# Two bottleneck layers in fp32: a Gram matrix whose pixels are transposed by transfers and VectorE instead of TensorE, a 3x3 row combination with four products, and filters made on GpSimd

## The chip, the cores and the metric

One core of one Trainium2 chip. The metric is device time in microseconds (us) of one execution, the median of several. Most executions of one kernel agree within 0.3%. The profiled span is some 2 us shorter than the timed run.

## The reference

Two equal layers act on x of 64 x 1024 x 14 x 14 fp32. The convolution biases and the residual scale are inputs (zero here, and softplus of zero is 0.69).

```python
def _bn(x, gamma, beta):
    mean = jnp.mean(x, axis=(0, 2, 3), keepdims=True)
    var = jnp.var(x, axis=(0, 2, 3), keepdims=True)
    ...
out = jax.nn.relu(_bn(_conv(x, w1, b1, 1, 0), g1, be1))     # 1x1, 1024 -> 256
out = jax.nn.relu(_bn(_conv(out, w2, b2, 1, 1), g2, be2))   # 3x3, 256 -> 256
out = _bn(_conv(out, w3, b3, 1, 0), g3, be3)                # 1x1, 256 -> 1024
out = jax.nn.softplus(residual_scale)[0] * out
return jax.nn.relu(x + out)
```

Each batch normalisation needs the statistics of all 64 images before anything can be normalised, so the work falls into stages: first convolution; 3x3 convolution of layer 0; its Gram stage; statistics, third convolution and residual of layer 0 fused with the first convolution of layer 1; 3x3 convolution and Gram stage of layer 1; its third convolution and residual.

## The kernel before

The mean and variance of the third convolution are not taken from its outputs. They follow from the Gram matrix (the products of every channel with every other, summed over pixels) of its 256 input channels over 12,544 pixels. For that product the kernel lays the pixels on the partitions, while the activations `y_all` have channels on the partitions. So TensorE transposes 98 chunks of 128 pixels, VectorE takes a constant off on the way out of PSUM, and TensorE multiplies.

```python
CH = 2;  NT = NPX // (CH * P);  NZT = 4       # two chunks of 128 pixels per step
FOUR = 3, 4                                   # row combinations with four products

def gram(psum, pool, aff, crow, beside):
    ...
    def products(k, zt):
        for c in range(CH):
            nc.tensor.matmul(g0, zt[:, c, 0:P], zt[:, c, :], ...)
            nc.tensor.matmul(g1, zt[:, c, P:M], zt[:, c, P:], ...)
    for k in range(NT):
        ...                                   # norms of the next image group (ScalarE)
        tp = psum.tile(CH * M)
        for c in range(CH):
            for s in range(MS):
                nc.tensor.transpose(tp[...], y_all[:, s, px], ident)
        zt = zts[k % NZT]
        nc.vector.tensor_tensor(zt[:, :, :M], tp..., crow..., ALU.subtract)
        if before is not None:
            products(*before)
        if k in beside:
            beside[k]()                       # layer 0: one piece of layer 1's filters
        before = k, zt
```

The 3x3 filters are turned into six row combinations, in four pieces per layer. Pieces of layer 0 are made during the first stage in a part of `y_all` not yet written; pieces of layer 1 during the Gram stage of layer 0, in two buffers borrowed from the pool that holds the x tiles.

```python
def filters(b, s, o, spare):
    first, second = spare
    ...
    nc.sync.dma_start(out=g, in_=w2s[b][:, s, o])            # SyncE loads the raw filter
    nc.vector.tensor_add(even, g[:, 0], g[:, 2])             # arithmetic: VectorE ...
    nc.scalar.activation(even, even, AF.Copy, scale=-1.0/6)  # ... and ScalarE
    ...
    nc.gpsimd.dma_start(out=us[b][i][:, s, o], in_=u)        # GpSimd stores each combination
```

The scheduler may move instructions when the program is built. SyncE's queue holds all loads of x. The kernel before gives the pieces of layer 0 two places in turn.

## Time and profile before

PE stands for TensorE's matmuls in the profile, PEld for its weight loads, DVE for VectorE, ACT for ScalarE, POOL for GpSimd, SP for SyncE, and a q after a name for that engine's queue. The granted clock is the share of full speed at which TensorE was let run. An issue is the instruction by which a queue starts a transfer, and the transfer lands when its data have arrived. A stage is measured from its first matmul to its last.

| stage (stretch of matmuls) | us |
|---|---|
| first convolution (ends at 310.99) | 305.3 |
| 3x3, layer 0 / layer 1 | 307.1 / 307.7 |
| Gram, layer 0 / layer 1 | 95.0 / 90.3 |
| statistics and fused stage | 625.0 |
| residual stage, layer 1 | 351.1 |
| kernel: 2118.75 (2117.68 to 2119.07), profiled span | 2116.9 |

The first lines are the busy tenths of TensorE and the granted clock in 40 slices of the span, from the page of the kernel before; the line after them is the first stage from its busy times by stretch, where the columns after the length are the busy times of PE, PEld, DVE, ACT and POOL, then the granted clock, the DMA share and GB/s.

```profile
PE   8999989999989999999999999899999899999999
...
PEclk9999999999999999999999999999999999999999
```

```profile
0.00:311.00 311.00, 302.10 (x904) 170.80 (x904) 194.20 (x273) 50.76 (x109) 13.79 (x30) 1.00 0.55 200
```

TensorE works through every slice at full clock.

### The profile page before, as it was taken

What the parts mean: (1) busy time and instruction counts of PE and PEld (TensorE: products, weight loads), DVE (VectorE), ACT (ScalarE), POOL (GpSimd) and SP (SyncE); (2) the same over time, 40 slices, a digit from 0 to 9 for tenths busy, and PEclk for the clock granted to TensorE, in tenths of its full rate; (3) what the DMA queues carried; (4) which work ended last, traced back from release to release, by engine and by line L of the source; (5) the groups of instructions that cost most, each with busy time, mean ns of one, the idle gap of its engine ahead of it and who ended that gap; (6) DMA issues with size and microseconds to landing.
All of it is one profiled execution on the core that took longest, in us unless ns stands there. A gap on an engine that the chain in (4) does not pass through costs nothing.

```text
span 2116.9 us, 27185 instructions
## 1 busy us (share of the span) xinstructions
PE 2068.3 (98%) x10368; PEld 1747.9 (83%) x10368; DVE 1433.2 (68%) x2778; ACT 814.2 (38%) x1579; POOL 243.5 (12%) x342
## 2 busy tenths in 40 slices
PE   8999989999989999999999999899999899999999
PEld 4555549999989889999999999799999897555555
DVE  5766559988866666666766667798888544444444
ACT  2211115233226055555555555523223402444444
POOL 0100000000001023333333333000000000000000
PEclk9999999999999999999999999999999999999999
DMA  7665425555543434444444443355554402778785
GB/s 292 250 211 209 163 90 192 201 191 184 200 159 118 155 150 159 177 183 161 175 160 176 183 160 145 120 214 184 190 208 180 194 1 99 306 277 325 282 321 215
DMA packets 45011, 400.00 MB, mean 189 GB/s; under 512 B 5584, under 2 KB 5840, under 8 KB 12240
## 3 DMA queue, kind: packets, MB, share of 16 engines
q1 hardware_dynamic: 30528, 280.28, 37.0%
q0 software_dynamic: 8448, 66.07, 7.7%
q10 hardware_dynamic: 5904, 51.91, 5.9%
q8 instruction: 82, 1.34, 0.3%
q14 instruction: 49, 0.40, 0.1%
HBM read 280.79 MB, written 117.44 MB: 188 GB/s over the span
## 4 chain that ended last, share of the span: by engine, by line
PE 93%; DVE 3%; ACT 2%; DMA 1%; issue 1%; POOL 0%; SPq 0%; DVEq 0%; ACTq 0%
PE ps L155 17%; PE ps L573 17%; PE ay L155 14%; PE ps L550 8%; PE cy L155 8%; PE ap L155 8%; PE ax L155 4%; PE cp L155 4%; PE ps L560 3%; PE cp L755 3%; PE cx L155 2%; PE ap L756 2%; ACT y L427 1%; PE ps L773 1%; DMA y<-in_w 0%
## 5 line engine op out<-in xcount | busy, mean ns | idle before, releaser
L573 PE MATMUL ps<-r,u 128*128 128x224 f32 (+1 forms) x2048 | 391.2, 343 | 14.1 <-DVE r L506 14.1
L573 PEld LDWEIGHTS ps<-r,u 128*128 128x128 f32 x2048 | 372.1, 190 | 18.9 <-DVE r L506 7.9
L155 PE MATMUL ps<-y,w 128*128 128x392 f32 x1024 | 340.5, 496 | 0.0
L155 PEld LDWEIGHTS ps<-y,w 128*128 128x128 f32 x1024 | 195.9, 191 | 143.5 <-issue 2.8
L837 DVE SCALAR_TENSOR_TENSOR x<-ps,scale,x 128x392 f32<-128x392 f32 x256 | 160.0, 626 | 175.5 <-PE ps L155 171.8
L265 ACT ACTIVATE cu<-cy,scale 128x196 f32<-128x196 f32 x372 | 154.0, 423 | 221.2 <-PE cy L155 221.2
L838 ACT ACTIVATE x<-x,shift 128x392 f32<-128x392 f32 x264 | 163.6, 622 | 183.7 <-DVE x L837 183.7
L155 PE MATMUL ay<-at,w1s 128*128 128x196 f32 (+1 forms) x752 | 209.7, 382 | 1.2 <-ACT au L265 1.0
L605 ACT ACTIVATE ms<-ps 128x448 f32<-128x448 f32 (+1 forms) x80 | 40.5, 506 | 333.7 <-PE ps L550 323.3
L155 PEld LDWEIGHTS ay<-at,w1s 128*128 128x128 f32 x752 | 136.0, 190 | 36.6 <-ACT au L265 4.6
L550 PE MATMUL ps<-sums,u 128*128 128x224 f32 (+1 forms) x768 | 158.6, 337 | 0.0
L265 ACT ACTIVATE x<-x,shift 128x392 f32<-128x392 f32 x248 | 140.9, 614 | 28.3 <-POOL x L399 28.3
L399 POOL TENSOR_TENSOR x<-x,cu 128x392 f32<-128x392 f32 x124 | 125.9, 1015 | 188.1 <-DVE x L373 188.0
L373 DVE SCALAR_TENSOR_TENSOR x<-cp,scale,x 128x196 f32<-128x196 f32 x248 | 103.4, 417 | 63.7 <-PE cp L155 63.7
L550 PEld LDWEIGHTS ps<-sums,u 128*128 128x128 f32 x768 | 131.5, 189 | 0.1
L155 PE MATMUL cy<-ct,w3s 128*128 128x196 f32 x496 | 123.0, 330 | 1.4 <-ACT cu L265 1.4
L755 PE MATMUL cp<-zt 128*128 128x257 f32 x392 | 120.6, 389 | 2.9 <-DVE zt L775 2.4
L265 ACT ACTIVATE au<-ay 128x196 f32<-128x196 f32 (+1 forms) x141 | 53.8, 381 | 167.2 <-PE ay L155 164.6
L155 PE MATMUL ap<-x,w1s 128*128 128x196 f32 (+1 forms) x376 | 107.7, 390 | 5.4 <-DVE y L311 5.4
L427 ACT ACTIVATE y<-y,shift,scale 128x1568 f32<-128x1568 f32 (+2 forms) x68 | 103.6, 1584 | 5.6 <-DVE shift L934 5.6
L155 PE MATMUL ax<-x,w 128*128 128x196 f32 (+1 forms) x376 | 104.8, 381 | 0.0
L155 PE MATMUL ay<-x,w 128*128 128x196 f32 (+1 forms) x376 | 104.8, 381 | 0.0
(226 smaller groups left out, 3429.2 us busy)
## 6 DMA issues: line engine op xcount, KB each, us to landing
x<-in_x SPq DMA_DIRECT2D x62, 1568.0 KB, 6.6
u<-u SPq DMA_DIRECT2D x64, 1280.0 KB, 5.5
x<-mid SPq DMA_DIRECT2D x32, 1568.0 KB, 7.6
mid<-x ACTq DMA_DIRECT2D x31, 1568.0 KB, 5.1
out<-x POOLq DMA_DIRECT2D x31, 1568.0 KB, 7.1
u<-u SPq DMA_DIRECT2D x32, 1024.0 KB, 4.8
u<-y POOLq DMA_DIRECT2D x16, 320.0 KB, 6.2
u<-spare POOLq DMA_DIRECT2D x16, 320.0 KB, 2.7
```

Source lines behind the costliest of these rows:

```text
L155: tc.keep_in_program_order(nc.tensor.matmul(*args, **kw))
L265: tc.keep_in_program_order(nc.scalar.activation(*args, **kw))
L373: nc.vector.scalar_tensor_tensor(v, bank, self.scale[:, o : o + 1], v, ALU.mult, ALU.add)
L399: nc.gpsimd.tensor_add(v, v, self.u12)
L427: nc.scalar.activation(y, y, AF.Relu, bias=shift[:, s : s + 1], scale=scale[:, s : s + 1])
L550: nc.tensor.matmul(to[:, o, :n], u[:, s, o, k], v[:, s].rearrange("p l c -> p (l c)"), start=(s == 0), stop=(s == MS - 1),)
L560: nc.tensor.matmul(to, u[:, s, o, k], v, start=(s == 0), stop=(s == MS - 1))
L573: nc.tensor.matmul(to, u[:, s, o, k], v, start=start, stop=stop, skip_group_check=by_slot)
L755: nc.tensor.matmul(g0, zt[:, c, 0:P], zt[:, c, :], start=first, stop=last)
L756: nc.tensor.matmul(g1, zt[:, c, P:M], zt[:, c, P:], start=first, stop=last)
L837: nc.vector.scalar_tensor_tensor(v, ps, scale[:, o : o + 1], v, ALU.mult, ALU.add)
L838: nc.scalar.activation(v, v, AF.Relu, bias=shift[:, o : o + 1])
```

## The change

Its intent: take 91 of the 98 chunk transposes off TensorE in each Gram stage. Sixteen transfers per tile of seven chunks rearrange 32-partition blocks within SBUF (block j of source i goes to block i, place j), and VectorE transposes inside 32x32 blocks. Besides that, the third row combination gets four products instead of five, the difference tiles of the 3x3 stages (differences of column halves, which a combination with four products needs) go to GpSimd, and so does all filter arithmetic. All four pieces of layer 0 now share one place. The core of the diff:

```diff
-CH = 2
-NT = NPX // (CH * P)
+CH0, CH = 7, 7
+QPX = (NPX - CH0 * P) // 4
+SPX = CH * P // 4
+NT = QPX // SPX                      # 13 tiles
-FOUR = 3, 4
+FOUR = 3, 4, 5
 def filters(b, s, o, spare):
     nc.sync.dma_start(out=g, in_=w2s[b][:, s, o])
-    ... (VectorE and ScalarE)
+    eng = nc.gpsimd
+    eng.tensor_tensor(even, g[:, 0], g[:, 2], ALU.add)
+    ... (31 more additions and scalings on eng)
-            nc.gpsimd.dma_start(out=us[b][i][:, s, o], in_=u)
+            eng.dma_start(out=us[b][i][:, s, o], in_=u)
-                    nc.vector.tensor_sub(diffs, r[:, :, :, :WH], r[:, :, :, WH:])
+                    nc.gpsimd.tensor_sub(diffs, r[:, :, :, :WH], r[:, :, :, WH:])
 def gram(...):
+        def spread(k):
+            px = slice(k * SPX, (k + 1) * SPX)
+            for s in range(MS):
+                norm(s, runs[:, s, :, px], aff)
+            to = sums_tile(homes, ("w1", "w3")[k % 2])...
+            for i in range(4):
+                for j in range(4):
+                    nc.sync.dma_start(
+                        out=to[32 * i : 32 * i + 32, :, j, :], in_=runs[32 * j : 32 * j + 32, :, i, px]
+                    )
+        def transposed(k, zd):
+            nc.vector.transpose(zt[:, :, :M]..., zd...)
+            nc.vector.tensor_sub(zt[:, :, :M], zt[:, :, :M], crow...)
...
-                if t % 4 == 2 and t // 4 < MS * MS:
+                if t % 6 == 2 and t // 6 < MS * MS:          # when a filter piece starts, first stage
```

## The prediction

> **What bounds the kernel now.** I read the page first: the busy line, then the chain of work that ended last.
>
> ```profile
> PE 2068.3 (98%) x10368; PEld 1747.9 (83%) x10368; DVE 1433.2 (68%) x2778; ACT 814.2 (38%) x1579; POOL 243.5 (12%) x342
> ...
> PE 93%; DVE 3%; ACT 2%; DMA 1%; issue 1%; POOL 0%; SPq 0%; DVEq 0%; ACTq 0%
> ```
>
> TensorE is busy for 98% of the span and holds 93% of the chain. So time is won by taking matmuls away, as long as nothing slower takes their place. The second view is busy time by stage. I cut it at the stage borders that the timeline shows: first convolution, 3x3 convolution of layer 0, its Gram stage, its statistics, the fused stage, then the same for layer 1 and the residual stage.
>
> ```profile
> 311.00:625.40 314.40, 307.08 (x1792) 304.83 (x1792) 273.00 (x534) 107.32 (x189) 0.00 (x0) 0.99 0.52 188
> 625.40:726.50 101.10, 91.68 (x589) 83.43 (x590) 63.05 (x137) 41.18 (x59) 13.09 (x28) 0.95 0.47 167
> ...
> 1665.80:1760.80 95.00, 89.41 (x589) 82.75 (x590) 37.91 (x65) 26.33 (x19) 0.20 (x4) 0.96 0.20 81
> ...
> 421.26:459.34 38.08, 38.08 (x225) 37.86 (x225) 32.70 (x62) 11.69 (x23) 0.00 (x0) 1.00 0.54 194
> ```
>
> After the length come the busy times of PE, PEld, DVE, ACT and POOL. The first three rows are a 3x3 stage and the two Gram stages; PE fills all three. The last row is one of the eight image groups of a 3x3 stage in steady state: 38.08 us, all PE, with VectorE at 32.70. GpSimd is idle in the 3x3 stages.
>
> The third view is the timeline inside a Gram stage, one period of two 128-pixel chunks:
>
> ```profile
> 1698.08 0.60 PE L773 MATMUL ps<-ident,y 128*128 128x128 f32 x4
> 1698.52 0.60 PE L755 MATMUL cp<-zt 128*128 128x257 f32 x2
> 1698.95 0.39 PE L756 MATMUL ap<-zt 128*128 128x129 f32 x2
> 1699.18 0.60 PE L755 MATMUL cp<-zt 128*128 128x257 f32 x2
> 1699.61 0.38 PE L756 MATMUL ap<-zt 128*128 128x129 f32 x2
> 1699.83 0.60 PE L773 MATMUL ps<-ident,y 128*128 128x128 f32 x4
> ```
>
> Read the starts, not the durations (matmuls overlap): the period is 1.75 us, of which the four transposes take 0.44 and the products 1.31, so 0.655 per chunk. 98 chunks make 85.8 us. By the timeline the stages' matmuls run from 631.47 to 726.48 and from 1670.50 to 1760.84.
>
> The fourth view is the DMA queue's own timeline, because the change issues many small transfers:
>
> ```profile
> 626.83 0.33 SPq L150 DMA_DIRECT2D w<-in_w  x1
> 627.21 0.43 SPq L1022 DMA_DIRECT2D crow<-in_par  x1
> 627.69 1.07 SPq L164 DMA_DIRECT2D spare<-in_w  x2
> ...
> out<-x SPq DMA_DIRECT2D x4, 392.0 KB, 2.5
> ```
>
> SyncE needs 0.33 us for an issue after a pause; back to back the starts lie 0.38 and 0.48 us apart. The last line is from the page: a small transfer out of SBUF lands 2.5 us after its issue.
>
> **What the Trainium skill says.**
> - "DMA: Bandwidth & Descriptors", Rules for kernel authors: transfers under 64 KB are mostly overhead. The new ones have 32 partitions x 2 x 896 B = 57 KB. Its section "Issuing engines are not separate DMA queues" calls the sequencer's issue time "usually small relative to the DMA itself"; the rows above put it at 0.4 us, which isn't small here.
> - "VectorE: DVE Perf Modes", The TRN2 errata: an fp32 tensor_tensor takes (N+151)/0.96 ns. The trace agrees: 617 ns for 448 elements (624 by the formula), 1083 ns for 896 (1091). The section "The three transpose paths" says that VectorE transposes only blocks of 32x32, at 311 ns for 128 columns of bf16; I take one element per cycle for fp32 too (an estimate; no run here shows it).
> - "GPSIMD Engine Reference", 3.1: GpSimd's tensor_tensor is about half as fast as VectorE's. The trace: 1015 ns for 392 elements on POOL, about 0.57 us on VectorE by the formula.
> - "TensorE: Matmul & The Clock Gate", Part 1: after an idle window the PE runs at half rate. The trace shows it: after 6.09 us of idleness at 631.47 the pair of cp matmuls takes 1.07 us, later 0.60.
>
> **The change part by part.**
>
> *3x3 stages.* A row combination with five products of 224 columns costs 7.22 us (2 x 3.61, the spacing of its rows in the chain); one with four costs 16 matmuls x 2 instructions x 224 columns x 0.855 ns (0.22 us for 257 columns above) = 6.13. The third combination goes from five to four: 1.09 us less in each of 8 groups and 2 stages, 17.4 us. The group then takes 36.99 us on PE. VectorE per group: three difference tiles move to GpSimd (two were on VectorE: -1.00), two pairs of 448 ns edge subtractions become single ones (-0.29), the new combination adds one subtraction of 768 elements (+0.95) and two shared parts (2 x 0.617 = +1.23). That makes +0.89, 33.6 us under 37.0: PE still bounds. GpSimd gets about 2.9 us per group, ScalarE two more edge copies. I take 17 us.
>
> *Filters on GpSimd.* In the first stage they free VectorE and ScalarE. The PE gaps there that end with VectorE add up to 1.2 us at 64.42 and 102.60: about -1 us. In the first Gram stage a piece costs, at 2.1 ns per element plus 0.19 for two inputs and about half of that for one, some 18 us plus six issues of 0.54, so 21 us; four make 84. They lie beside the stage. They hold the x buffers that the statistics and the first residual tiles need; the third should be done about when the stage ends, the fourth before its buffer is needed.
>
> *Gram stages.* Removed from PE: 91 of 98 chunks x 0.22 = 20.0 us each; the PE floor is 98 x 0.655 + 7 x 0.22 = 65.7 us. Added, for each of 13 tiles of seven chunks (4.6 us of products): 2 norms on ScalarE of about 1.1 us, a transpose and a subtraction of 1792 elements on VectorE, (1792+151)/0.96 = 2.02 us each, so 4.05; and **16 transfers, all from SyncE**: 208 issues per stage. For SyncE to keep up with 4.6 us, an issue could take 0.29 us. It takes 0.37 to 0.48. So the bound moves from PE to SyncE's issues. Eight transfers at most are in flight (each issue waits for the landing of the eighth before it); 2.5/8 = 0.31 us stays below.
>
> The end of the stage: the first spread can start after six norms (from the 256- and 1568-element rows, 592 and 1683 ns, I get 2 x (0.59 + 0.91 + 1.13) = 5.3 us), at 1669.85 + 5.3 = 1675.1. I choose 0.40 us per issue, between first and steady spacing, since each transfer has half the descriptors of those measured: 208 x 0.40 = 83.2, plus 2.5 landing, 4.05 VectorE, 4.6 products: 1769.4, which is 8.6 us later than now. Layer 0: 630.73 + 5.3 + 94.3 = 730.3, plus about 3 for two filter loads in the same queue and the weight combinations at the end of the stage: 733.3, 6.8 later. Together +15.4.
>
> *Sum:* -17 - 1 + 15.4 = -2.6. The transposes removed give nothing, since the issues replace them; the 3x3 stages' gain is mostly eaten. Because a change that somebody wrote out in full was probably seen to help, I lean a little to the cheap side of the issue: 2112 us.
>
> **The rivals.**
> 1. *PE stays the bound in the Gram stages* (issues cost 0.29 us or less). Then the stages end after 5.3 + 4.6 + 2.5 + 4 + 13 x 4.6 = 76 us: 706 + 3 and 1746, so -17 and -15, and the kernel takes about 2118.75 - 32 - 18 = 2069. For it: half the descriptors per transfer. Against: no issue in the trace is under 0.32 us, with any size.
> 2. *Issues cost the full back-to-back 0.46 us.* 208 x 0.06 = 12.5 us more per stage: 2140. For it: 0.46 to 0.48 is what follows the second of any row of transfers.
> 3. *PE cools.* With 2 us or more of idleness in each 6.4 us the clock may fall to half: 9.2 us per tile in place of 6.4, up to 36 us per stage, 2150 to 2185. Against: the idle time is shorter than the 6 us after which the trace shows the slow rate, and a PE at half rate is busy all the time and warms again.
> 4. *VectorE bounds the 3x3 stages*: the first group of each is already fully busy on VectorE (38.09 us). It would cost a few us, not the gain.
> 5. *GpSimd's filters are late* and hold back x buffers: 0 to 10 us after the first Gram stage.
>
> **Range and chances.** The cost of an issue spans 0.37 (2103) to 0.46 (2140); rivals 1, 3 and 5 widen both ends: 2082 to 2144. Over 2% faster needs 2076 or less, thus an issue near 0.3 us: 8%. Over 2% slower (above 2161) needs rival 3 or issues over 0.5 us: 6%. Within 2%: 86%.
>
> **What would show it.** In the 3x3 stages a group should take 37.0 us with PE at 100%. In the Gram stages the DMA queue's timeline should be one unbroken row of issues 0.40 us apart, PE busy about 65 of 95 to 100 us, its gaps ended by VectorE's subtraction, and that waiting in turn for landings. The chain of waits should show the SyncE queue or the transfers for some 8% of the span. I am wrong if PE's products follow each other without gaps there (rival 1), if the granted clock falls to half inside the stage (rival 3), or if statistics or residual tiles wait for u<-spare.

## The result, and the profile after

The changed kernel takes 2278.2 us (2277.3 to 2280.56, 4 runs) against 2118.91 of the kernel before in the same rounds: ratio 1.0752, 95% interval 1.0733 to 1.0771. Here and below a ratio and its interval are from the fast runs of both kernels in the same rounds, so a ratio is not quite that of the medians quoted. It is 7.5% slower, where I had given that side 6%, and 134 us above the top of the range.

From the page of the changed kernel: the busy line, TensorE and clock in slices, and the chain of work that ended last, by engine and by line.

```profile
PE 2064.1 (91%) x9876; PEld 1728.9 (76%) x9876; DVE 1476.4 (65%) x2602; ACT 799.0 (35%) x1555; POOL 588.9 (26%) x642
...
PE   8469998999985679999999999899999567999999
...
PEclk9789999999997789999999999999999788999999
...
PE 77%; SPq 11%; POOL 4%; DMA 3%; DVE 2%; issue 1%; ACT 1%; ACTq 0%; DVEq 0%; POOLq 0%
PE ps L162 15%; PE ay L162 12%; PE ps L586 12%; SPq L781 11%; PE ps L563 8%; PE cy L162 7%; PE ap L162 7%; PE ps L573 5%; PE ax L162 4%; PE cp L162 4%; POOL y L176 2%; PE cx L162 2%; DMA x<-in_x 1%; DMA u<-y 1%; DMA y<-in_w 1%
```

TensorE has 492 matmuls fewer and is busy hardly less, because part of its time passes at a lower clock (0.93 in the first stage, about 0.8 in the Gram stages, in the rows below). The chain, once 93% PE, now holds 11% of one line of SyncE's queue, L781, the 416 new transfers, and 4% of GpSimd. Three places in the slices are thin: near the start, after some 30%, and at some 80%. The stretches of the same stages as before show them:

```profile
0.00:362.80 362.80, 307.98 (x904) 174.25 (x904) 181.37 (x209) 36.24 (x69) 135.99 (x158) 0.93 0.47 171
362.80:668.40 305.60, 298.25 (x1728) 295.92 (x1728) 286.51 (x526) 111.02 (x205) 56.32 (x24) 0.99 0.52 186
668.40:831.90 163.50, 94.59 (x407) 80.94 (x408) 69.70 (x57) 29.72 (x32) 109.29 (x136) 0.79 0.51 150
1764.60:1920.10 155.50, 92.01 (x407) 78.48 (x408) 59.72 (x50) 29.66 (x31) 0.15 (x2) 0.80 0.39 109
```

The 3x3 stage (second row) shrank as foreseen. The first stage is 52 us longer with the same matmuls. In the Gram stages PE is busy about 60% of the time, at a granted clock of 0.8. In stretches of matmuls, the sum is 159 us, all of the difference of the spans:

| stage | before | after | moved | predicted |
|---|---|---|---|---|
| first convolution, end | 311.0 | 362.8 | +51.8 | -1 |
| 3x3, both | 614.8 | 595.9 | -18.8 | -17.4 |
| Gram, layer 0 | 95.0 | 157.4 | +62.4 | +6.8 |
| Gram, layer 1 | 90.3 | 150.7 | +60.3 | +8.6 |
| statistics and fused | 625.0 | 628.4 | +3.4 | 0 |
| residual, layer 1 | 351.1 | 351.1 | 0 | 0 |

**Inside a Gram stage.** Rows of the changed kernel's timeline: start, length, engine, line, operation, out<-in and count; in brackets how long the engine was idle and what ended it.

```profile
1836.70 10.21 SPq L781 DMA_DIRECT2D w1s<-y  x16
...
1837.81 2.05 DVE L788 STREAM_TRANSPOSE zt<-w3s 128x1792 f32<-128x1792 f32 x1 [6.27 <-DMA w3s<-y]
...
1839.89 2.02 DVE L792 TENSOR_TENSOR zt<-zt,crow 128x1792 f32<-128x1792 f32 x1
...
1841.97 0.73 PE L770 MATMUL cp<-zt 128*128 128x257 f32 x2 [3.53 <-DVE zt L792]
...
1847.02 1.22 SPq L781 DMA_DIRECT2D w3s<-y  x2
```

SyncE needs 10.21 us for the 16 issues of one tile, 0.64 us each from start to start, and 0.1 us later begins the next tile. PE waits for VectorE, VectorE for the landing, the landing for the issues. VectorE's 2.05 and 2.02 us are what I estimated (2.02 each). The first issues of 13 successive tiles in layer 1 lie 10.49 us apart in the mean, (1899.4 - 1773.5) / 12.

**Inside the first stage.** SyncE's queue between 59 and 101 us, then its waits in the first 200 us (us in total, times, longest), then two of VectorE's and TensorE's there.

```profile
59.55 0.33 SPq L172 DMA_DIRECT2D y<-in_w  x1
59.98 0.85 SPq L121 DMA_DIRECT2D x<-in_x  x2
99.93 0.33 SPq L172 DMA_DIRECT2D y<-in_w  x1
100.35 0.86 SPq L121 DMA_DIRECT2D x<-in_x  x2
```

```profile
SPq L172 <- POOL y L176: 92.7, 3, 36.2
```

```profile
DVE at L334 <- DMA x<-in_x: 52.0, 3, 21.3
...
PE ap L162 <- DVE y L324: 46.9, 3, 19.7
```

L172 is the load of a filter piece into the spare part of `y_all`. It waits until GpSimd is done with the piece before, three times and 92.7 us in all. The x loads stand behind it in the same queue and go out within half a microsecond of it. VectorE then waits for x, and TensorE for VectorE: three long gaps, 47 us. The piece before matters because all pieces share one place; two places with the load left in SyncE's queue were not tried.

### The profile page after: what moved, and what is told of

It is laid out like the page before. It is cut to its first block, busy times and chain, and to the rows that moved or that the text cites. A ratio compares the mean times of both kernels' runs of the same rounds, so it can differ in the third digit from the quotient of the medians.

```text
span 2275.7 us, 26888 instructions
## 1 busy us (share of the span) xinstructions
PE 2064.1 (91%) x9876; PEld 1728.9 (76%) x9876; DVE 1476.4 (65%) x2602; ACT 799.0 (35%) x1555; POOL 588.9 (26%) x642
## 4 chain that ended last, share of the span: by engine, by line
PE 77%; SPq 11%; POOL 4%; DMA 3%; DVE 2%; issue 1%; ACT 1%; ACTq 0%; DVEq 0%; POOLq 0%
PE ps L162 15%; PE ay L162 12%; PE ps L586 12%; SPq L781 11%; PE ps L563 8%; PE cy L162 7%; PE ap L162 7%; PE ps L573 5%; PE ax L162 4%; PE cp L162 4%; POOL y L176 2%; PE cx L162 2%; DMA x<-in_x 1%; DMA u<-y 1%; DMA y<-in_w 1%
## 5 line engine op out<-in xcount | busy, mean ns | idle before, releaser
L586 PE MATMUL ps<-r,u 128*128 128x224 f32 (+1 forms) x1536 | 293.7, 343 | 14.1 <-DVE r L519 14.1
L586 PEld LDWEIGHTS ps<-r,u 128*128 128x128 f32 x1536 | 279.3, 190 | 18.1 <-DVE r L519 7.9
L491 POOL TENSOR_TENSOR diffs<-r 128x336 f32<-128x336 f32 (+1 forms) x48 | 115.3, 2405 | 647.3 <-DVE r L471 459.5
L770 PE MATMUL cp<-zt 128*128 128x257 f32 x392 | 153.8, 481 | 121.3 <-DVE zt L792 120.1
L770 PEld LDWEIGHTS cp<-zt 128*128 128x128 f32 x392 | 77.1, 244 | 127.1 <-DVE zt L792 125.0
L162 PE MATMUL ap<-x,w1s 128*128 128x196 f32 (+1 forms) x376 | 114.0, 409 | 51.2 <-DVE y L324 51.2
L875 POOL DMA_DIRECT2D out<-x x31 | 16.5, 532 | 479.6 <-ACT x L872 479.6
L573 PE MATMUL ps<-v,u 128*128 128x168 f32 (+1 forms) x768 | 131.1, 322 | 0.0
L162 PEld LDWEIGHTS ap<-x,w1s 128*128 128x128 f32 x376 | 68.1, 198 | 81.0 <-DVE y L324 55.8
```

The costliest lines, as they stand in the source:

```text
L162: tc.keep_in_program_order(nc.tensor.matmul(*args, **kw))
L491: nc.gpsimd.tensor_sub(diffs, r[:, :, :, :WH], r[:, :, :, WH:])
L573: nc.tensor.matmul(to, u[:, s, o, k], v, start=(s == 0), stop=(s == MS - 1))
L586: nc.tensor.matmul(to, u[:, s, o, k], v, start=start, stop=stop, skip_group_check=by_slot)
L770: nc.tensor.matmul(g0, zt[:, c, 0:P], zt[:, c, :], start=first, stop=last)
```

## The experiments

"Gram0" and "Gram1" are the Gram stages of layer 0 and layer 1. All numbers of stages are stretches of matmuls as in the table above.

### third_comb_only: the kernel before, with the 3x3 part of the change alone

```diff
 (kernel before)
-FOUR = 3, 4
+FOUR = 3, 4, 5
+ (the 3x3 stage's code of the change; filters and Gram stages as before)
```

> The kernel before with only the change of the 3x3 stages: third row combination with four products, difference tiles on GpSimd; filters and Gram stages as before. Theory (the 3x3 part gains by itself what it gains in the changed kernel): both 3x3 stages 9 to 10 us shorter, Gram stages 95 and 90 us as before, 2100 us, ratio 0.991. Rival (the difference tiles on GpSimd, 2.4 us each, or VectorE hold PE back and part of the gain is lost once the stages next to it are not slowed): 2108 to 2119.

Measured: 2127.82 us (2127.57 to 2128.96), ratio 1.0038 (1.0023 to 1.0053). The expected total was missed. The 3x3 stages do shrink by 18.5 us (298.5 and 297.8), but the first stage grows from 305.3 to 333.0 us. Its timeline, at the first of four such places:

```profile
53.97 0.42 ACT L191 ACTIVATE y<-y 128x256 f32<-128x256 f32 x1 [2.27 <-DVE y L190]
...
55.25 0.47 ACT L265 ACTIVATE au<-ay 128x392 f32<-128x392 f32 x1
...
55.78 5.47 PE L155 MATMUL ay<-at,w1s 128*128 128x392 f32 x8 [4.74 <-ACT au L265]
```

PE had finished `ay` at 51.0 us. ScalarE copies it out (L265) only at 55.25, because filter scalings (L191) stand before it in ScalarE's queue and wait for VectorE. PE idles for 4.74 us, and its next eight matmuls take 5.47 us where the eight before took 2.80: the granted clock is 0.51 there and was 1.00 before. The four-product filter has more small steps that go back and forth between the two engines. So the 3x3 gain is real and was given back in another stage.

### filters_back: the changed kernel, with the filters on VectorE and ScalarE again

```diff
 (changed kernel)
-    eng = nc.gpsimd ...            (the change's filters)
+    ... the kernel before's filters, started at t % 4 == 2
```

> The changed kernel with the filters back on VectorE and ScalarE with their old schedule. Theory (the first stage's 52 us come from the filters on GpSimd): first stage ends near 311 us in place of 363, Gram stages stay near 157 and 151 us, 2226 us. Rival (the first stage is longer for another reason, such as the tiles laid out anew): above 2265.

Measured: 2255.18 us (2251.49 to 2256.22), ratio 1.0633; the first stage takes 334.1 us, not 305. It removes only 23 us of the 52, for the reason of the run above: this is the same four-product filter on the same two engines, and its trace has the same four waits of 4.74 us for ScalarE. Taken together the two runs say that neither place of the arithmetic is free as it stands. They do not yet tell whether GpSimd's slowness or SyncE's queue costs the 52 us.

### load_on_gpsimd: the filter loads leave SyncE's queue

```diff
 (changed kernel)
-        nc.sync.dma_start(out=g, in_=w2s[b][:, s, o])
+        nc.gpsimd.dma_start(out=g, in_=w2s[b][:, s, o])
```

> The changed kernel with the filters still on GpSimd, but their four loads per layer issued by GpSimd itself in place of SyncE. Theory (the load of a piece waits in SyncE's queue for the piece before, 37 us of GpSimd and 8 us of landing, and the loads of x behind it wait too): the first stage ends near 311 us, 2226 us, though GpSimd is as slow as before. Rival (GpSimd's reads and writes of SBUF slow VectorE and so PE): first stage stays near 363 us, 2270 us or more.

Measured: 2221.64 us (2219.62 to 2226.07), ratio 1.0482. The first stage in busy times by stretch, to be held against the row of the changed kernel:

```profile
0.00:311.40 311.40, 301.81 (x904) 171.30 (x904) 182.99 (x209) 36.07 (x70) 148.26 (x162) 1.00 0.56 199
```

GpSimd is busy no less (148 us, 136 in the changed kernel), and the last filter piece is done at about the same time (179 us against 187), yet the stage is back at 305.3 us of matmuls and full clock. One line's engine decides 51.5 us. So it was not the slow arithmetic by itself: it was a load that waits for that arithmetic, at the head of the queue that feeds TensorE. This is the shown cause of the first stage's +52.

### two_queues: the Gram transfers alternate between SyncE and ScalarE

```diff
 (changed kernel)
-                    nc.sync.dma_start(
+                    (nc.sync if j % 2 == 0 else nc.scalar).dma_start(
```

> The changed kernel with every second transfer of the Gram stages issued by ScalarE. Theory (the bound is 0.64 us of the issuing sequencer for each transfer, and each sequencer pays for its own): per tile SyncE 8 x 0.64 = 5.1 us, ScalarE 8 x 0.64 + 2.2 of norms = 7.3 us in place of 10.3; the Gram stages shrink from 157 and 151 us to 110 to 120, total about 2200 us. Rival (both sequencers share one generator of descriptors, or the transfers themselves are the bound): no tile under 10 us, total 2270 or more.

Measured: 2217.56 us (2217.29 to 2218.66), ratio 1.0461. Gram1 falls from 150.7 to 100.0 us, better than expected. The timeline there:

```profile
1805.54 5.08 SPq L781 DMA_DIRECT2D w1s<-y  x8
1805.54 5.42 ACTq L781 DMA_DIRECT2D w1s<-y  x8
...
1811.01 2.16 ACT L440 ACTIVATE y<-y,shift,scale 128x896 f32<-128x896 f32 x2 [4.47 <-DMA w1s<-y]
...
1812.17 1.23 SPq L781 DMA_DIRECT2D w3s<-y  x2
```

Both queues issue eight transfers in the same 5 us, so each sequencer pays its own price and nothing common to them stands in the way. ScalarE's norms (1811.01) start right after its own last issue (1805.54 + 5.42), and the next tile starts after the first norm: 6.6 us per tile. Gram0 only falls to 149 us. There SyncE's queue shows filter loads at 711.31 and 740.71 between the spreads, waiting for GpSimd as in the first stage, with 23.5 and 28.9 us from the start of one spread to the next. So the total lies above the 2200 us expected.

### both_queues_fixed: the two repairs together

> The changed kernel with the two repairs of load_on_gpsimd and two_queues together: filter loads issued by GpSimd, Gram transfers alternately by SyncE and ScalarE. First stage 305 us, Gram stages 100 to 110 (no filter loads in SyncE's queue among the spreads) and 100 us. Sum 2278 - 52 - 50 - 50 = about 2127 us (2120 to 2140), if the two causes are separate and additive. Rival: the layer-0 Gram stage stays at 149 us as in two_queues, because GpSimd's filters and not SyncE's queue hold it: about 2170.

Measured: 2146.18 us (2143.32 to 2147.65), ratio 1.0119. First stage 305.5 and Gram1 99.9, as expected. Gram0 is 117.3 us against 149.1 in two_queues, so the loads in SyncE's queue had held it; it remains 17 us above Gram1, and why stays open. But the stage after Gram0 is 638.8 us, 12 more than in load_on_gpsimd. The sum is 19 us above what I expected; what eats it is told with four_transfers below.

### issue_shapes: the disputed cost by itself

A small kernel with groups of 16 transfers of one form each; it copies x to the output. Its output is wrong, which doesn't matter for the time.

```diff
+a: nc.sync.dma_start(out=a[:, 0, k],     in_=x[1][:, ...224])       # HBM to SBUF, 128 partitions x 896 B
+b: nc.sync.dma_start(out=b[:, 0, k],     in_=src[:, k % 2, ...224]) # the same within SBUF
+c: nc.sync.dma_start(out=c[:32, 0, k],   in_=src[:32, k % 2, ...])  # 32 partitions, one run
+d: nc.sync.dma_start(out=d[:32, :, k],   in_=src[:32, :, ...])      # 32 partitions, two runs
+e: nc.sync.dma_start(out=e[32:64, :, k], in_=src[:32, :, ...])      # as d, to other partitions: the change's form
+f: nc.sync.dma_start(out=f[:, :, k],     in_=src[:, :, ...])        # 128 partitions, two runs
+i, j: as d, from ScalarE and from GpSimd           (g, h, l are left out here)
```

> No timing of the kernel; eleven groups of 16 small transfers, result wrong on purpose (x copied to out). The question is what makes one SyncE issue of the Gram transfers 0.60 us busy and 0.64 us start to start where the kernel before shows 0.33 to 0.43. Theory A, the number of runs (two runs of 896 bytes per partition): the one-run groups a (from HBM, 128 partitions), b (within SBUF, 128) and c (within SBUF, 32) cost about 0.40 us each, the two-run groups d, e (32), f (128), g (64) about 0.6. Theory B, SBUF as the source: a 0.40, everything else 0.6. Theory C, partitions and so descriptors: cost grows with partitions, f about twice d or more, c the cheapest. Group e (to another quadrant) equals d if crossing partitions costs nothing at the issue. i (ScalarE) and l (alternating) pay 0.6 per sequencer; j (GpSimd) is unknown, 0.6 to 1.0.

Each line gives the shortest, median and longest issue in ns:

```profile
L49 SPq DMA_DIRECT2D a<-in_x x16: 328/430/711, 1.2 to 9.5; - x16
L52 SPq DMA_DIRECT2D b<-src x16: 533/599/602, 12.2 to 21.8; - x16
L55 SPq DMA_DIRECT2D c<-src x16: 507/589/591, 24.5 to 33.9; - x16
L58 SPq DMA_DIRECT2D d<-src x16: 586/596/672, 36.5 to 46.6; - x16
L64 SPq DMA_DIRECT2D f<-src x16: 627/634/686, 61.6 to 71.8; - x16
```

My theory A, two runs per partition, falls: one run (c) costs as much as two (d). So does theory C: 128 partitions and two runs (f) cost 6% more than 32 partitions (d), for four times the bytes. The change's own form (e) takes 596 ns, as d does. Theory B stands: a and b have one shape and differ in the source alone, 430 against 599 ns (start to start 0.47 against 0.64 us, outside one pause in a). A store from SBUF to HBM, `out<-x` in the kernel before, takes SyncE 335 ns, so SBUF as the source is not enough by itself; that store has another shape, so it is likely, and not shown, that both ends must lie in SBUF. Every row of my profile before had one end in HBM. ScalarE pays 618 ns (i), GpSimd 533 ns (j).

### eight_transfers and four_transfers: the same bytes in fewer issues

Built on load_on_gpsimd; SyncE alone issues. The pixels land in wrong places. The comparison with the reference still passed within its tolerance, so a pass does not tell whether a Gram stage puts its pixels right, in these runs or in any other.

```diff
 eight_transfers
+            for i in range(2):
+                for j in range(4):
+                    nc.sync.dma_start(out=to[64*i : 64*i+64, :, j, :],
+                                      in_=runs[64*(j%2) : 64*(j%2)+64, :, j, px])
 four_transfers
+            for j in range(4):
+                nc.sync.dma_start(out=to[:, :, j, :], in_=runs[:, :, j, px])
```

> load_on_gpsimd with the same bytes of each Gram tile moved by SyncE alone in 8 transfers of 64 partitions instead of 16 of 32; the pixels land in wrong places, so the result is wrong on purpose. Theory (the number of issues bounds the tile): 8 x 0.64 = 5.1 us plus the 1.5 us that two_queues also had left over per tile, 6.6 us a tile; layer-1 Gram stage 100 us instead of 150, layer-0 100 to 117 instead of 153; kernel about 2146 us, as both_queues_fixed (2135 to 2155). Rival (bytes or landing bound the tile): nothing changes, 2221 us.

> The same bytes in 4 transfers of 128 partitions; wrong on purpose again. Theory: 4 x 0.68 = 2.7 us plus 1.5 is below the 4.6 us of products, so PE bounds the tile and the layer-1 Gram stage takes about 80 us, as gram_three_queues; layer 0, with GpSimd's filters beside it, 85 to 105; kernel about 2110 us (2095 to 2125). Rival: 2221 us, or a floor of about 100 us per stage from landing and norms (6.6 us a tile whatever the count): 2146 us.

Measured: eight_transfers 2130.31 us (ratio 1.0047, below my 2135 to 2155), Gram0 96.2, Gram1 86.1; four_transfers 2120.49 us (ratio 1.0004), Gram0 79.5, Gram1 76.3. With eight, most tiles of Gram1 take 5.28 us, the time of the eight issues and hardly more; the leftover of 1.5 us that I had carried over from two_queues is not there, because ScalarE no longer issues between its norms. With four, PE bounds. The timeline of four_transfers in Gram1:

```profile
1709.88 2.62 SPq L780 DMA_DIRECT2D w1s<-y  x4
...
1714.48 2.61 SPq L780 DMA_DIRECT2D w3s<-y  x4
...
1716.97 2.05 DVE L785 STREAM_TRANSPOSE zt<-w1s 128x1792 f32<-128x1792 f32 x1 [0.49 <-PE ap L771]
```

The spreads lie 4.60 us apart, the time of a tile's products, and VectorE now waits for PE. Same bytes, same VectorE work, one queue: mostly 10.3, 5.3 and 4.6 us a tile with 16, 8 and 4 issues. That the count of issues bounded the changed kernel's Gram stages is shown.

The stage times fell by 148 us against load_on_gpsimd's two Gram stages, and the kernel only by 101. In four_transfers the stage after Gram0 takes 674.1 us instead of 626.5. The waits between 702 and 780 us:

```profile
DVE q L845 <- DMA u<-spare: 31.5, 1, 31.5
PEld ay L162 <- DVE q L845: 30.7, 1, 30.7
PE ay L162 <- DVE q L845: 29.9, 1, 29.9
```

VectorE needs a buffer that still holds the layer-1 filters which GpSimd is making (`spare`), and PE waits with it. The four pieces end at 772, 773 and 774 us in four_transfers, eight_transfers and both_queues_fixed, whatever their Gram0 takes (79, 96, 117), and Gram0 plus the stage after it is 753.6, 755.8 and 756.1 us in the three.

### four_transfers_one_piece: the buffers come free

```diff
 (four_transfers)
-beside = {1 + 3 * i: partial(piece, i // MS, i % MS) for i in range(MS * MS)}
+beside = {1: partial(piece, 0, 0)}        # one piece, stored to all four places: wrong on purpose
```

> four_transfers, but GpSimd makes only one of the four layer-1 filter pieces beside the layer-0 Gram stage and stores it to all four places (wrong on purpose). In four_transfers, eight_transfers and both_queues_fixed the four pieces end at 772 to 774 us of the span whatever the Gram stage takes (79, 96 and 117 us), and the stage that follows starts late by 47, 33 and 12 us because two of its x buffers are lent to them. If that is what eats the rest: Gram stage 79 us, following stage back from 674 to 627 us, kernel about 2073 us (2066 to 2080). Rival: the following stage is longer for another reason (the clock after a dense Gram stage, weights w1s and w3s shared with the moved pixels), and the kernel stays above 2100.

Measured: 2067.91 us (2067.26 to 2071.08), ratio 0.9763 (0.9746 to 0.9779). Gram0 79.5 and the next stage 625.0 us. The rival falls: neither the clock nor the shared buffers of `w1s` and `w3s` made that stage long. GpSimd's filters did. (This kernel is faster than the one before, and its result is wrong.)

### filters_gpsimd_old_gram and gram_three_queues: what of the change can be kept

```diff
 filters_gpsimd_old_gram = third_comb_only, plus
+    layer-0 filters on GpSimd, their loads issued by GpSimd, pieces at t % 6 == 2
 gram_three_queues = filters_gpsimd_old_gram, plus, in layer 1 only
+    the change's Gram stage, with
+    WHO = [0, 1, 0, 1, 2, 1, 0, 1, 0, 1, 2, 1, 0, 1, 2, 0]
+    (nc.sync, nc.gpsimd, nc.scalar)[WHO[4 * i + j]].dma_start(...)
```

> The kernel before, plus the four-product third combination with its layer-0 filters on GpSimd, whose loads GpSimd issues itself; both Gram stages as before. The first stage is 305 us as in load_on_gpsimd (not 333 as in third_comb_only, because ScalarE's queue has no filter work), 3x3 stages -18.8 us in sum, Gram stages 94 and 91. Sum about 2101 us (2096 to 2106), 0.9% faster than before. Rival: the old layer-0 Gram stage, with its layer-1 filters on VectorE and ScalarE, is disturbed by the four-product filter, +5 to +15 us there: 2106 to 2116.

> filters_gpsimd_old_gram with the new Gram stage in layer 1 only, its 16 transfers per tile issued 6 by SyncE, 7 by GpSimd and 3 by ScalarE. If only the issues bounded the new Gram stage: SyncE 6 x 0.64 = 3.8 us a tile, ScalarE 3 x 0.64 + 2 x 1.1 = 4.1, below the 4.6 us of products, so the stage takes about 75 us (70 to 80) instead of 91, and the kernel about 2085 us. Rival: GpSimd's issues cost about 1 us each, 7 us a tile, and the stage stays at 95 to 100 us: about 2107 us. Second rival, the clock: products back to back are granted half speed as the throttle answers, and the stage stays at 85 or more with PE gaps gone.

Measured: filters_gpsimd_old_gram 2100.4 us (2099.27 to 2101.29), ratio 0.9907 (0.9892 to 0.9922), as expected: first stage 305.0, 3x3 298.5 and 297.7, Gram stages 94.4 and 90.8. gram_three_queues 2093.01 us (2091.87 to 2094.24), ratio 0.9872 (0.9858 to 0.9887). Gram1 falls from 90.8 to 80.3 us, just above my 70 to 80; GpSimd's 7 issues take 3.7 us a tile, so the rivals of slow issues on GpSimd and of the clock both fall, but the total I named (2085) was missed by 8 us. Of these, 5 are in the stage (75 expected, 80.3 measured), and the residual stage after it takes 352.7 instead of 349.4 us. The traces say where: in its first 36 us the granted clock is 0.86 instead of 0.95, and PE is busy throughout in both; after that the two are alike (944 matmuls in 310 us at clock 1.00). Why the clock is lower there stays open. Both kernels lie below both of the given ones. Against the kernel before this is less than 2%, but the intervals exclude 1. The new Gram stage was kept out of layer 0 because GpSimd's filters might set the end there; with the layer-1 filters on VectorE and ScalarE, as in these two kernels, that was not tried.

## Why the prediction was wrong

The place where it went wrong is the one that I had named as the risk; the size was far off, and a second loss was not seen at all.

- **3x3 stages, -17.4: right.** -18.8 in the changed kernel, -18.5 alone; a group takes 36.97 us, where 36.99 was worked out. VectorE does not bound them, so rival 4 is out: 286.5 of 305.6 us busy. Some parts of the working were off without a cost. A difference tile on GpSimd takes 2.4 us in the mean, where my "about 2.9 us per group" allowed about 1 us each; VectorE is busy 34.3 to 34.9 us per group, not 33.6; and the matmuls of the five-product row are of 224 and 192 columns by turns, but its 7.22 us were measured.
- **Filters on GpSimd, "about -1 us" in the first stage: the failed step, +51.8 us there.** I counted what VectorE and ScalarE are spared, and no wait: the piece's load stayed in SyncE's queue, waits for the piece before, and holds up x. load_on_gpsimd takes away just that, and the 52 us with it. The arithmetic was mis-sized too. A piece was put at 21 us, for the first Gram stage; GpSimd is busy for 31.0 us with each there (123.9 us of its rows between 668 and 850 us, over four pieces) and for 34.6 in the first stage (138.3). The term at fault is "about half of that for one": a scaling of 384 elements, with one input, takes 1.29 us in Gram0 in the mean, an addition with two 1.10. load_on_gpsimd, where GpSimd is as busy, shows that this alone costs the first stage nothing.
- **Gram stages, +15.4: the mechanism was right, the size of one term was not.** The bound moved from PE to SyncE's issues, as said. "I choose 0.40 us per issue" was the failed term: it is 0.64. 208 x 0.24 = 50 us per stage, of the 52 (layer 1) and 56 (layer 0) by which the two stages exceed my figures; in layer 0 another 4 go away with the filter loads (load_on_gpsimd, 153.3 us). The 0.40 came from transfers with one end in HBM, and I argued that half the descriptors could only make it cheaper. issue_shapes shows that four times the partitions cost 6% more, and that transfers within SBUF cost more than those from HBM. The error of the range has the same source: its ends, 0.37 and 0.46, were both taken from the wrong kind of transfer, and no term of it stood for the first stage.
- **Rival 1** (PE stays bound, Gram stage 76 us, kernel 2069) is what four_transfers and four_transfers_one_piece show once the issues are few and the buffers free: 76.3 and 2067.9 us. The arithmetic of TensorE's saving was right, though only kernels with wrong results reach it here.
- **Rival 2** (0.46 us) had the direction right, and fell short for the same reason.
- **Rival 3** (PE cools) happened, against my reason for ruling it out: after 3.53 us of idleness at 1841.97 a pair of products takes 1.06 us, and 0.60 some 4 us later. In Gram1 nine of the 13 tiles go so, after 3.53 to 10.83 us of idleness; the four after 2.51 to 2.96 us take 0.60 from the second pair on. The Trainium skill has it, in "TensorE: Matmul & The Clock Gate", Part 1 (one idle window of about 3.4 us), and the tiles of Gram1 agree; I had used the 6 us that the trace of before happened to show. It costs little in the changed kernel, since PE waits for issues anyway.
- **Rival 5** (filters late, 0 to 10 us) did not happen in the changed kernel, where the Gram stage itself was slow: the +3.4 us of the stage after it come with a lower granted clock in its first 40 us (0.87 instead of 0.96, PE busy 37.48 us in both). Once the Gram stage is mended, the filters cost 47 us. A repair of the issues alone could therefore never have brought the full gain.

The +159 us is thus explained: first stage +52 (shown by load_on_gpsimd), Gram stages +123 (shown by the count of issues), 3x3 stages -19. The statistics and fused stage adds the +3.4. Left open are why the clock is lower at the start of some stages that follow a Gram stage, what holds Gram0 in both_queues_fixed, and why an issue with both ends in SBUF is dearer.

## What to carry to other kernels

Price a new transfer by a transfer of the same kind, with the same two memories at its ends; where the trace has none, measure sixteen of them before building on them, and count issues rather than bytes. Before moving work to a slower engine, ask which queue still holds an instruction that waits for it, and what stands behind that instruction. When the first bound is repaired, look at once for what was hidden behind it: here borrowed buffers cost nothing until the Gram stage became short.

## What the Trainium skill lacked or had wrong

- "DMA: Bandwidth & Descriptors", Issuing engines are not separate DMA queues: it calls the sequencer's time "usually small relative to the DMA itself" and gives no figure by the kind of transfer. Here an issue within SBUF takes SyncE 0.60 us (0.64 start to start), ScalarE 0.62 and GpSimd 0.53, from HBM to SBUF 0.43, and the transfer lands after 2.0 us. 208 of them in a stage made 133 us. Its remark that several issuing engines save only sequencer time agrees, and that time was worth 51 us in Gram1 here (two_queues) and 36 in Gram0 (both_queues_fixed against load_on_gpsimd).
- "GPSIMD Engine Reference", 4.1 Engine selection: it calls operations with one input "roughly line-rate" on GpSimd. In the changed kernel a scaling of 128x384 fp32 takes 1.76 us in the mean in the first stage, beside a busy VectorE, and 1.29 in Gram0; an addition with two inputs of that size takes 1.09 and 1.10. One input is not the cheaper case.
